# Attention with a gated mixture of experts: the exponentials of the shortest tiles transposed by TensorE, the loads of x placed three units later, four buffers for stored projections

## The chip, the core and the metric

The kernel runs on one NeuronCore of a Trainium2 chip. The core has a matrix engine (TensorE, PE in the profile; PEld is its loading of weights), a vector engine (VectorE, DVE), a scalar engine (ScalarE, ACT), a general engine (GpSimd, POOL) and a queue engine (SyncE, SP). Each works through its own queue of instructions in order. They meet through semaphores only. DMA transfers are issued from the queues of SP, ACT and POOL and run on 16 DMA engines. Matmuls write to PSUM, a memory of eight banks; everything else lies in SBUF or in the chip's main memory (DRAM).

The metric is the device time of one execution in microseconds (us), the median over several. Lower is better. The profile is that of one execution, and all times within it are counted from the start of its span.

## What is computed

```python
xn = layernorm(x)                      # x: (2, 2048, 512), float32
# attention, one head, on xn
x_norm = (xn - mu) / sqrt(var + EPS) * gamma + beta
q, k, v = x_norm @ qkv[:, :512], x_norm @ qkv[:, 512:1024], x_norm @ qkv[:, 1024:]
scores = where(causal, q @ k.T / sqrt(512), -inf)
s = softmax(scores) @ v @ o_proj + xn
# mixture of 8 experts, 2 for each token, on xn (hidden size 352)
top_scores, top_idx = top_k(xn @ gate_w.T + gate_b + bias, 2)
comb = one_hot(top_idx) weighted by softmax(top_scores)
h = silu(xn @ w1[e].T + b1[e]);  y = h @ w2[e].T + b2[e]
g = silu(sum over e of comb[e] * y[e])
return x + s * g
```

## The kernel before

**Stages.** The 4096 tokens are 32 tiles of 128 rows, in eight batches of four. The kernel has three stages, one after the other, all in float32.

The first stage folds the weights (the product of the query and key weights, and that of the value and output weights, L207), normalises each batch (`norm_stats`, `norm_rows`), makes its keys (`keys`, with the transposed rows zT), its gating scores (`both`, `keep_scores`), and from the keys two projections, one for the queries and one for the values. The projections of the first five batches are made by seven products instead of eight (`seven_products`), and those of the last three by plain `unit`s: four matmuls into one of four PSUM banks (`ps_p`), a copy by ScalarE into a buffer of the pool `stg` (L351), and a store to DRAM on ScalarE's queue (L352). Keys and projections go to DRAM. At the end of the stage the tokens are routed (`route`): VectorE counts and sorts with the help of a few small matmuls (L525, L596), with constants that GpSimd has made (from L454 on).

The second stage is the experts: 68 slots of tokens are gathered, transposed by DMA, multiplied (L879), put through silu, transposed, and multiplied again (L918).

The third stage is attention, a loop over steps s. Tile `seq[s]` is the query tile of step s; the causal mask gives it (t + 1) x 128 keys, where t is its place in its sequence of 16 tiles. The order is t = 15, 14, ... 0 for the first sequence and 8, 9, 0, 1, 6, 7, 2, 3, 4, 5, 10 to 15 for the second. `widths[s]` cuts the keys into chunks of up to 512. In step s:

- PE makes the scores of tile s, one PSUM bank of the five of `ps_a` for each chunk (`chunk_scores`, L963). VectorE takes each chunk's maximum (L969), and then nm, the negative of the largest (L981, in `end_scores`).
- ScalarE makes the exponentials pr with nm as bias (`exponentials`, L1035), which also sums them.
- The values of a tile need these exponentials transposed (pT, keys on the partitions). [...]GpSimd copies pr to pu, the two halves of every number apart (L1039); SP issues the DMA transpose (L1044); and in the next step VectorE joins the halves into pT (`join_p`, L1051).
- PE multiplies pT of tile s - 2 with the values (`values`, L1069) in the same step, behind the scores. Some pairs of tiles (`FAST`, the first eight steps' tiles and the last six's) take a form with seven products instead (L1122).
- ScalarE scales the result (`attended`, L1237), VectorE adds to it (L1240), the expert outputs are gathered by GpSimd (`gather_y`, L1216), weighted by VectorE (`gate`, L1227 and L1228) and put through silu by ScalarE (L1232), and GpSimd multiplies and adds (`emit`, L1248 and L1249). Between an exponential and a silu ScalarE loads another table.

**What sets the order.** The whole order is written out by hand: each engine carries out its instructions in the order in which the program text issues them. In the first stage a table, `between`, says after which unit a step of the normalisation comes: `put(at - STEP + 1, norm_rows, b)` places `norm_rows` of batch b. STEP is 6. At its end `norm_rows` issues four DMA loads of x for batch b + 2 on SP's queue (`load`, L160); x has two buffers. Waits come from the buffers: a buffer, a PSUM bank or a place in memory that another tile had before is written only when the last use of that tile is done.

Of the kernel before, what the change touches and what calls it, by code (L numbers as in the profile page):

```python
# [10 lines left out]
F32 = mybir.dt.float32  # L11
# [9 lines left out]
P = 128  # L21
# [5 lines left out]
def gated_attention_moe(  # L27
# [27 lines left out]
    nc = tc.nc  # L55
# [3 lines left out]
    NT = B * S // P  # L59
    BT = 4  # L60
    TB = BT * P
    NB = NT // BT
    NBB = S // TB
# [31 lines left out]
    ident = const.tile([P, P], F32, name="ident")  # L95
# [34 lines left out]
    stage_a = ExitStack()  # L130
    right = lambda st, **k: st.enter_context(tc.tile_pool(side="right", **k))
    psum = lambda st, **k: st.enter_context(tc.tile_pool(space=PSUM, **k))
    kp = right(stage_a, name="kp", bufs=BT)
    mp = right(stage_a, name="mp", bufs=1)
    stg = right(stage_a, name="stg", bufs=3)
    ps_p = psum(stage_a, name="ps_p", bufs=ND)

    wqk = mp.tile([P, ND, D], F32, name="wqk")
# [18 lines left out]
    def load(b):  # L157
        xt = xp.tile([P, BT, D], F32, name=f"x_{b}", tag="x")
        for t in range(BT):
            nc.sync.dma_start(out=xt[:, t, :], in_=xb[:, b * BT + t, :])  # L160
        xin[b] = xt
# [58 lines left out]
    def norm(b):  # L220
        norm_stats(b)
        norm_rows(b)
# [20 lines left out]
    def norm_rows(b):  # L243
        xt = xin.pop(b)
        mv, va, rs = stats.pop(b)
        zs = []
        for t in range(BT):
            z = zp.tile([P, D], F32, name=f"z_{b}_{t}", tag="z")
            nc.vector.tensor_scalar(  # L249
                z, xt[:, t, :], mv[:, t, 0:1], rs[:, t, 1:2], ALU.subtract, ALU.mult  # L250
            )
            zs.append(z)

        ratio = sm.tile([P, BT, 1], F32, name=f"ratio_{b}", tag="ratio", bufs=4)
        nc.vector.tensor_tensor(ratio, va[:, :, 1:2], rs[:, :, 1:2], ALU.mult)
        nc.vector.tensor_tensor(ratio, ratio, rs[:, :, 0:1], ALU.mult)
        nc.vector.tensor_copy(xscale[:, ts(b, BT)], rs[:, :, 0])
        nc.vector.scalar_tensor_tensor(
            xshift[:, ts(b, BT)], mv[:, :, 0], -1.0, rs[:, :, 0], ALU.mult, ALU.mult
        )  # L260
        ratios[b] = ratio
        for t in range(BT):
            zu = zus[t]
            nc.gpsimd.tensor_copy(  # L264
                zu[:, : 2 * D].rearrange("p (h d) -> p h d", h=2),
                zs[t].bitcast(U16).rearrange("p (d h) -> p h d", h=2),
            )
            nc.gpsimd.tensor_copy(zu[:, 2 * D : 2 * D + 2], ratio[:, t, :].bitcast(U16))
            if b >= BY_TE:
                zuT = zup.tile([P, 2 * ND, P], U16, name=f"zuT_{b}_{t}", tag="zuT", bufs=BT + 2)  # L270
                nc.sync.dma_start_transpose(out=zuT, in_=zu[:, : 2 * D])
                zuts[b, t] = zuT
            nc.sync.dma_start(out=zu_rows[:, b * BT + t, :], in_=zu)
        zs_of[b] = zs
        if b + 2 < NB:
            load(b + 2)

    def keys(b):
# [405 lines left out]
    def put(i, f, *args):  # L684
        between.setdefault(i, []).append((f, args))

    STEP = 6
# [3 lines left out]
    for b in range(1, NB):  # L691
        at = LAST - 5 - STEP * (NB - 1 - b) if b > 1 else 1
        put(at, keys, b)
        put(at + 3, both, b)
        put(at + (5 if b == NB - 1 else 7), keep_scores, b)
        if b > 1:

            put(max(at - STEP - 1, 0), norm_stats, b)
            put(at - STEP + 1, norm_rows, b)
    for e in range(E):  # L700
        put(LAST - 5 + e, load_w1, e)

# [249 lines left out]
    widths, scored, halves, turned, sums, gates, outs = {}, {}, {}, {}, {}, {}, {}  # L952
# [38 lines left out]
    ps_a = psum(att, name="ps_a", bufs=5)  # L991
# [13 lines left out]
    for i in range(NS):  # L1005
        experts_step(i)
        if i >= 8 and i % 2 == 0 and early:
            f, b, c = early.pop(0)
# [14 lines left out]
    tp = left(name="tp", bufs=3)  # L1023
# [4 lines left out]
    def exponentials(s):  # L1028

        _, nm, chunks = scored.pop(s)  # L1030
        rs = sm.tile([P, NBB], F32, name=f"rs_{s}", tag="rs")
        sums[s], halves[s] = rs, []
        for j, w in enumerate(widths[s]):
            pr = pp.tile([P, TB], F32, name=f"pr_{s}_{j}", tag="pr")
            nc.scalar.activation(  # L1035
                pr[:, :w], chunks[j][:, :w], AF.Exp, bias=nm, accum_out=rs[:, j : j + 1]
            )
            pu = php.tile([P, 2 * TB], U16, name=f"pu_{s}_{j}", tag="pu")
            nc.gpsimd.tensor_copy(  # L1039
                pu[:, : 2 * w].rearrange("p (h d) -> p h d", h=2),  # L1040
                pr[:, :w].bitcast(U16).rearrange("p (d h) -> p h d", h=2),
            )
            puT = php.tile([P, 2 * BT, P], U16, name=f"puT_{s}_{j}", tag="puT", bufs=5)
            nc.sync.dma_start_transpose(out=puT[:, : 2 * w // P, :], in_=pu[:, : 2 * w])  # L1044
            halves[s].append(puT)

    def join_p(s, j):
        w = widths[s][j]
        if j == 0:
            turned[s] = tp.tile([P, NBB * TB], F32, name=f"pT_{s}", tag="pT")  # L1050
        nc.vector.tensor_copy(  # L1051
            turned[s][:, j * TB : j * TB + w].bitcast(U16).rearrange("p (i t h) -> p i t h", t=P, h=2),
            halves[s][j][:, : 2 * w // P, :].rearrange("p (h i) t -> p i t h", h=2),
        )

    def values(s):
        po = ps_b.tile([P, D], F32, name=f"po_{s}", tag="b")
        product(po, s, 0, place_keys(s), slice(0, D))
        outs[s] = po

    def place_keys(s):

        return place(s)[1] + 1 + (place(s)[0] - place(s)[2]) * BT

    def product(dst, s, k0, k1, cols, start=True):

        first = place(s)[2]
        for k in range(k0, k1):
            nc.tensor.matmul(  # L1069
                dst, lhsT=turned[s][:, ts(k, P)], rhs=avs[first + k // BT][:, k % BT, cols],  # L1070
                start=(start and k == k0), stop=(k == k1 - 1),
            )
# [223 lines left out]
    for s in range(NT + OUT + 2):  # L1296
        fast = s // 2 - 1 in FAST
        if s < NT and s:
            begin_scores(s)
        if s == 1:  # L1300
            fetch_parts(s, 2 * ND)
        for k in range(NT):
            if k not in AHEAD:
                wait = 4 - k % 2 if k // 2 in FAST else 3
                if s == k + wait:
                    attended(k)
                if s == k + wait + 1:
                    emit(k)
        for k in range(NT):
            if s == (NT - 1 if k in AHEAD else k + 2 - k % 2 if k // 2 in FAST else k + 1):  # L1310
                fetch_inputs(k)
        joins = []
        if 0 <= s - 1 < NT - 1:
            joins = [(join_p, s - 1, j) for j in range(len(widths[s - 1]))]
        if s < NT:
            for j in range(len(widths[s])):
                if s:
                    chunk_scores(s, j)
                if joins:
                    f, *args = joins.pop(0)  # L1320
                    f(*args)
                if s == 2 and j:
                    for b in (0, 1) if j == 1 else (j,):
                        combine_v(b, (1,))
        for f, *args in joins:
            f(*args)
        if s < NT and s:
            end_scores(s)
        if fast and s % 2 == 0 and s < NT:
            combine_p(s - 2, range(NBB) if s == 2 else ())  # L1330
        if 0 <= s - 1 < NT:
            divisor(s - 1)
        if s < NT:
            exponentials(s)
            fetch_parts(s, 4 if s else 2 * ND)
            if s in combine:
                combine_v(combine[s])
        if fast and s % 2 == 0:
            values_first(s - 2)

            if s != NT - 2:
                values_next(s - 2)
        elif fast and s == NT - 1:
            values_next(s - 3)
            gate(s - 1)
            values_end(
                s - 3,
                [lambda j=j: join_p(s, j) for j in range(len(widths[s]))] + [lambda: combine_p(s - 1)],
            )
            for k in AHEAD:  # L1350
                make_ahead(k)
        elif fast:
            values_end(s - 3)
        elif 0 <= s - 2 < NT:
            values(s - 2)

        for k in range(0, NT - 2, 2):
            if s == (k + 2 if k + 2 in AHEAD else k + 3):
                gate(k)
        for k in range(0, NT, 2):  # L1360
            if s == (k if k in AHEAD else k + 1):
                gather_y(k)
                gather_y(k + 1)
# [45 lines left out]
```

## Time and profile before

| | |
|---|---|
| Median of 3 runs | 1072.64 us (1067.35, 1072.64, 1072.9) |
| Profiled execution | 1072.68 us, of which the span is 1071.0 |
| PE busy (98% of the span) | 1051.0 us |
| DVE, POOL, ACT busy | 598.7, 422.1, 310.6 us |
| Units of the last three batches | about 177 to 261 us |
| Experts | about 261 to 616 us |
| Steps 12 to 25 of attention | about 806 to 926 us |
| One plain copy of a projection (L351) | 586 ns, 24 of them |
| One copy of pr (L1039) | 1042 ns, 80 of them |
| DMA transpose of pu, issue to landing | 2.3 to 5.8 us, median 3.2 |
| One join (L1051) | 684 ns (283 to 2198), 80 of them |

Busy time is the sum of an engine's instructions. A wait in the profile is idle time of an engine before an instruction, with the one that released it; for instructions with several semaphores it is the one that came last. A float32 matmul is recorded as two, so eight records are four matmuls. Times of PE's ends are modelled: the distance from one start to the next says more than a length.

### The profile page before, as it was taken

How to read it: one execution, taken by the hardware profiler on the slowest of the kernel's cores; microseconds unless marked ns; L12 is line 12 of the kernel's file. 1: busy time of each engine (PE TensorE's matmuls, PEld its weight loads, DVE VectorE, ACT ScalarE, POOL GpSimd, SP SyncE). 2: the span in 40 equal slices, each digit the busy share in tenths (PEclk: the TensorE clock that was granted, in tenths of full speed). 3: DMA queues.
4: the chain of work that ended last, by engine and by line, in shares of the span. 5: the costliest groups of instructions: out<-in, count | busy, mean ns of one | idle time of the engine just before them, and what ended most of it. 6: DMA issues, size and time to landing. Idle time of an engine off the chain costs nothing.

```text
span 1071.0 us, 12108 instructions
## 1 busy us (share of the span) xinstructions
PE 1051.0 (98%) x3566; PEld 620.9 (58%) x3566; DVE 598.7 (56%) x1181; ACT 310.6 (29%) x659; POOL 422.1 (39%) x463
## 2 busy tenths in 40 slices
PE   8999999999999999999999999999999999999998
PEld 3687886444555555555545446776664444446677
DVE  5797884775333333333345338535555667675756
ACT  3212221211322232322355121312333343332330
POOL 2363240003433333333331023244557677574452
PEclk9999999999999999999999999999999999999999
DMA  8599989936999999999985186355668777763451
GB/s 305 170 282 280 276 257 335 351 123 176 225 222 234 226 227 227 232 226 224 214 187 131 42 224 145 91 122 156 154 176 231 219 201 207 202 171 91 108 141 40
DMA packets 303775, 210.11 MB, mean 196 GB/s; under 512 B 237784, under 2 KB 250840, under 8 KB 302688
## 3 DMA queue, kind: packets, MB, share of 16 engines
q1 hardware_dynamic: 284512, 146.91, 55.1%
q0 software_dynamic: 10560, 35.17, 13.1%
q10 hardware_dynamic: 8640, 27.27, 7.1%
q8 instruction: 30, 0.49, 0.2%
q14 instruction: 33, 0.27, 0.1%
HBM read 92.89 MB, written 60.03 MB: 143 GB/s over the span
## 4 chain that ended last, share of the span: by engine, by line
PE 65%; issue 13%; POOL 8%; DMA 5%; DVE 5%; SPq 2%; ACT 2%; ACTq 0%; POOLq 0%; DVEq 0%
PE ph L879 15%; PE py L918 15%; PE ps L963 13%; PE p L1122 10%; PE p L400 5%; PE pw L207 3%; DMA puT<-pu 2%; PE p L1069 2%; POOL yg L1216 2%; POOL pu L1039 1%; DMA zuT<-zu 1%; POOL o L1249 1%; POOL o L1248 1%; PE po L1069 1%; POOL zu L264 1%
## 5 line engine op out<-in xcount | busy, mean ns | idle before, releaser
L963 PE MATMUL ps<-k,q 128*128 128x512 f32 (+3 forms) x640 | 239.1, 529 | 0.0
L963 PEld LDWEIGHTS ps<-k,q 128*128 128x128 f32 x640 | 117.7, 190 | 122.0 <-issue 112.1
L918 PE MATMUL py<-w,ht 128*128 (+3 forms) x408 | 187.0, 594 | 0.0
L879 PE MATMUL ph<-w,xT 128*128 (+1 forms) x544 | 173.2, 460 | 0.7 <-POOL keep L1001 0.7
L1039 POOL COPY pu<-pr 128x1024 uint16<-128x1024 uint16 (+3 forms) x80 | 85.1, 1092 | 176.1 <-ACT pr L1035 158.1
L926 DVE COPY y<-py 128x512 f32<-128x512 f32 x68 | 46.9, 690 | 177.4 <-PE py L918 177.4
L879 PEld LDWEIGHTS ph<-w,xT 128*128 128x128 f32 (+1 forms) x544 | 97.5, 181 | 74.1 <-issue 35.2
L904 ACT ACTIVATE ht<-ht,b1sel 128x128 f32<-128x128 f32 (+3 forms) x237 | 73.1, 375 | 231.8 <-DVE ht L898 231.8
L889 POOL COPY hu<-h 128x704 uint16<-128x704 uint16 x68 | 52.3, 769 | 206.8 <-ACT h L887 145.5
L918 PEld LDWEIGHTS py<-w,ht 128*128 128x128 f32 (+3 forms) x408 | 73.5, 182 | 75.4 <-issue 37.4
L765 POOL DMA_INDIRECT xs<-zu_d,toki x68 | 69.1, 1017 | 75.7 <-DVE toki L642 64.3
L1035 ACT ACTIVATE pr<-ps,nm 128x512 f32<-128x512 f32 (+3 forms) x80 | 49.1, 621 | 151.3 <-DVE ri L1200 136.1
L1069 PE MATMUL po<-v,pT 128*128 128x512 f32 x182 | 82.9, 603 | 5.8 <-DVE ri L1200 3.3
L969 DVE TENSOR_REDUCE mx<-ps 128x1 f32<-128x512 f32 (+3 forms) x80 | 48.6, 608 | 67.3 <-PE ps L963 66.0
L1216 POOL DMA_INDIRECT yg<-y_d,posi x64 | 66.8, 1044 | 38.4 <-DVE g L1227 21.0
L1051 DVE COPY pT<-puT 128x1024 uint16<-128x1024 uint16 (+3 forms) x80 | 61.0, 770 | 25.6 <-DMA puT<-pu 25.4
L264 POOL COPY zu<-z 128x1024 uint16<-128x1024 uint16 x32 | 35.2, 1100 | 80.3 <-DVE z L249 80.3
L1069 PEld LDWEIGHTS po<-v,pT 128*128 128x128 f32 x182 | 34.7, 194 | 45.8 <-issue 43.0
L413 DVE TENSOR_TENSOR so<-p,so 128x512 f32<-128x512 f32 x70 | 46.0, 686 | 15.7 <-PE p L400 7.4
L1240 DVE SCALAR_TENSOR_TENSOR o<-xo,xscale,o 128x512 f32<-128x512 f32 x30 | 27.4, 925 | 47.2 <-ACT o L1237 39.6
L839 DVE COPY xT<-xhT 128x1024 uint16<-128x1024 uint16 x68 | 46.8, 688 | 12.2 <-DMA xhT<-xs 7.1
L1248 POOL TENSOR_TENSOR o<-o,g 128x512 f32<-128x512 f32 x30 | 40.4, 1348 | 14.7 <-DVE o L1240 14.5
(216 smaller groups left out, 1443.8 us busy)
## 6 DMA issues: line engine op xcount, KB each, us to landing
y_d<-y SPq DMA_DIRECT2D x68, 256.0 KB, 3.7
zu_d<-zu SPq DMA_DIRECT2D x32, 264.0 KB, 5.4
x<-in_x_dram SPq DMA_DIRECT2D x32, 256.0 KB, 4.8
kt_d<-kT ACTq DMA_DIRECT2D x8, 1024.0 KB, 6.0
k<-kt_d SPq DMA_DIRECT2D x32, 256.0 KB, 4.4
q<-qt_d SPq DMA_DIRECT2D x32, 256.0 KB, 3.9
v<-v_d SPq DMA_DIRECT2D x32, 256.0 KB, 5.0
xo<-in_x_dram SPq DMA_DIRECT2D x32, 256.0 KB, 3.8
```

The lines of the kernel that those rows point to most:

```text
L400: nc.tensor.matmul(ps[:, r, :], lhsT=lhs[:, c, ts(r, P)], rhs=rhs[:, c, :], start=(c == 0), stop=(c == 1),)
L765: nc.gpsimd.indirect_dma_start(out=xs, out_offset=None, in_=zu_d, in_offset=bass.IndirectOffsetOnAxis(ap=toki[:, i : i + 1], axis=0),)
L879: nc.tensor.matmul(ph[at, :], lhsT=xT[:, c, at], rhs=rhs[k], start=(c == 0), stop=(c == ND - 1),)
L889: nc.gpsimd.tensor_copy(hu[:, :, :H], h.bitcast(U16).rearrange("p (d h) -> p h d", h=2))
L904: nc.scalar.activation(ht[:hn, c, at], ht[:hn, c, at], AF.Silu, bias=b1sel[:hn, c, j : j + 1])
L918: nc.tensor.matmul(py[at, :], lhsT=ht[:k, c, at], rhs=rhs[n], start=(c == 0), stop=(c == NH - 1),)
L963: nc.tensor.matmul(ps[:, :w], lhsT=aqs[seq[s] // 2][:, c, ts(t % 2, P)], rhs=aks[first + j][:, c, :w], start=(c == 0), stop=(c == ND - 1),)
L1039: nc.gpsimd.tensor_copy(pu[:, : 2 * w].rearrange("p (h d) -> p h d", h=2), pr[:, :w].bitcast(U16).rearrange("p (d h) -> p h d", h=2),)
L1051: nc.vector.tensor_copy(turned[s][:, j * TB : j * TB + w].bitcast(U16).rearrange("p (i t h) -> p i t h", t=P, h=2), halves[s][j][:, : 2 * ...
L1069: nc.tensor.matmul(dst, lhsT=turned[s][:, ts(k, P)], rhs=avs[first + k // BT][:, k % BT, cols], start=(start and k == k0), stop=(k == k1 - 1),
L1122: nc.tensor.matmul(dst, lhsT=a[:, k], rhs=v(k), start=(k == 0), stop=(stop and k == n - 1))
L1216: nc.gpsimd.indirect_dma_start(out=y, out_offset=None, in_=y_d, in_offset=bass.IndirectOffsetOnAxis(ap=posi[k][:, n : n + 1], axis=0),)
```

## The change

Three edits.

1. In attention, tiles of at most 384 keys (steps 13, 14, 15, 18, 19 and 22) leave out the copy by GpSimd, the DMA transpose and the join. Their exponentials stay where they are, and PE transposes them block by block with a matmul against the identity into a bank of `ps_a`, behind the values of the tile before; ScalarE copies the bank to pT. The other tiles stay as they are.
2. The loads of x for batch b + 2 (b from 2 on) are no longer issued at the end of `norm_rows`, but by an entry of the table three units later.
3. The pool `stg` has four buffers instead of three.

```diff
-    stg = right(stage_a, name="stg", bufs=3)
+    stg = right(stage_a, name="stg", bufs=4)
...
         zs_of[b] = zs
-        if b + 2 < NB:
+        if b < 2:
             load(b + 2)
...
             put(at - STEP + 1, norm_rows, b)
+            if b + 2 < NB:
+                put(at - STEP + 4, load, b + 2)
...
                 pr[:, :w], chunks[j][:, :w], AF.Exp, bias=nm, accum_out=rs[:, j : j + 1]
             )
+            if by_te(s):
+                halves[s].append(pr)
+                continue
             pu = php.tile([P, 2 * TB], U16, name=f"pu_{s}_{j}", tag="pu")
...
+    def by_te(s):
+        return sum(widths[s]) <= 3 * P
+
+    def turn_p(s):
+        n = sum(widths[s])
+        pt = ps_a.tile([P, TB], F32, name=f"pt_{s}", tag="a")
+        for k in range(n // P):
+            nc.tensor.transpose(pt[:, ts(k, P)], halves[s][0][:, ts(k, P)], ident)
+        turned[s] = tp.tile([P, NBB * TB], F32, name=f"pT_{s}", tag="pT")
+        nc.scalar.copy(turned[s][:, :n], pt[:, :n])
...
-        if 0 <= s - 1 < NT - 1:
+        if 0 <= s - 1 < NT - 1 and not by_te(s - 1):
             joins = [(join_p, s - 1, j) for j in range(len(widths[s - 1]))]
...
         elif 0 <= s - 2 < NT:
             values(s - 2)
+            if s - 1 < NT and by_te(s - 1):
+                turn_p(s - 1)
```

## The prediction

> **What bounds the kernel now.** First the page's busy times, then every wait of the matmul queue over the whole run (who waited for whom: us in total, times, longest).
>
> ```profile
> PE 1051.0 (98%) x3566; PEld 620.9 (58%) x3566; DVE 598.7 (56%) x1181; ACT 310.6 (29%) x659; POOL 422.1 (39%) x463
> ```
> ```profile
> PE po L1069 <- DVE ri L1200: 3.3, 1, 3.3
> PE po L1069 <- DVE pT L1051: 2.5, 3, 1.5
> ```
>
> TensorE sets the end: it idles 20 us of 1071.0, and 5.8 of these are four waits of one line, the product of weights and values (L1069). The rest of the idle time lies in the head, in the tail and before the first tiles of attention. What is not on PE's queue, or does not end one of its waits, is worth nothing. So I read PE's order of time (start, length, work, idle before it and its releaser) around those four waits:
>
> ```profile
> 826.43 1.05 PE L963 MATMUL ps<-k,q 128*128 128x128 f32 x8
> 830.80 4.36 PE L1069 MATMUL po<-v,pT 128*128 128x512 f32 x6 [3.32 <-DVE ri L1200]
> 835.00 7.92 PE L963 MATMUL ps<-k,q 128*128 128x512 f32 x24
> ...
> 855.48 7.99 PE L1069 MATMUL po<-v,pT 128*128 128x512 f32 x18 [0.49 <-DVE pT L1051]
> ...
> 865.71 8.82 PE L1069 MATMUL po<-v,pT 128*128 128x512 f32 x20 [0.51 <-DVE pT L1051]
> ...
> 913.03 2.74 PE L1069 MATMUL po<-v,pT 128*128 128x512 f32 x6
> ...
> 922.39 3.67 PE L1069 MATMUL po<-v,pT 128*128 128x512 f32 x8 [1.46 <-DVE pT L1051]
> ```
>
> The six records at 830.80 are the values of tile 13 (three key blocks, two records each). They wait 3.32 us, and then run slowly: 4.20 us until the next scores start, where the six at 913.03 take 2.58 (next start 915.61). The table of stages (PE, weight loads, DVE, ACT, POOL, granted clock, DMA) shows why:
>
> ```profile
> 830.00:834.00 4.00, 3.20 (x4) 1.51 (x5) 1.58 (x5) 2.52 (x4) 1.52 (x3) 0.57 0.79 293
> 918.00:922.00 4.00, 2.93 (x11) 1.71 (x9) 2.74 (x3) 0.00 (x0) 3.43 (x4) 1.00 0.93 322
> ```
>
> After 3.32 us idle the clock was 0.57; in the wait of 1.46 us it stayed 1.00. So the first wait costs 3.32 + 1.62. All four cost 3.32 + 1.62 + 0.49 + 0.51 + 1.46 = 7.40 us. What ends the first is on VectorE and ScalarE:
>
> ```profile
> 826.55 0.42 DVE L969 TENSOR_REDUCE mx<-ps 128x1 f32<-128x256 f32 x1
> 829.11 1.54 DVE L1051 COPY pT<-puT 128x768 uint16<-128x768 uint16 x1 [2.14 <-DMA puT<-pu]
> 830.58 0.14 DVE L981 TENSOR_REDUCE nm<-mx 128x1 f32<-128x1 f32 x1
> ```
> ```profile
> 830.79 1.28 ACT L1035 ACT_TABLE_LOAD   x1 [5.33 <-DVE ri L1200]
> 832.55 0.77 ACT L1237 ACTIVATE o<-po,xshift,ri 128x512 f32<-128x512 f32 x1
> ```
>
> VectorE holds tile 14's maximum at 826.97, but its in-order queue stands at the join of tile 13 (L1051) until that tile's DMA transpose lands; so the join delays PE, and also nm, the exponential of tile 14, and all behind it.
>
> [...]
>
> **The change by parts.**
>
> *x loaded later.* Sixteen DMAs (four for each of batches 4 to 7) move three units on in the text. In the order of the built program they do not move: on SP's queue they stand behind the same store and before the same transposes, since those three units give SP nothing; every queue and every wait value up to the routing is as before. Zero, with no cover needed.
>
> *Four buffers for stored projections.* In 177 to 261 us ScalarE's copies (L351) waited for their earlier stores 7.5 + 6.7 us, and 6.8 for a load[...]. PE waited for none of it: the copies go through four PSUM banks, and PE runs without a gap from 166 to 261. Zero now; at most the one ACT-bound gap at 261.77, 0.7 us, if the last copy came sooner, which it doesn't (it waits for its matmul). But the buffer shifts the memory of the stage's other pools, and with it a wait: POOL's first routing memset (L454) then waits for the transposes of the last gating scores (L322) instead of the last keys.
>
> ```profile
> 174.85 0.54 POOL L454 MEMSET rank<- 128x32 f32 x8 [16.41 <-ACT kT L295]
> 177.02 0.14 POOL L469 IOTA tile_i<- 128x32 int32 x1
> 180.48 0.60 PE L322 MATMUL pgt<-ident,part 128*128 128x128 f32 x4
> 180.92 7.03 PE L341 MATMUL pj<-kT,wqk 128*128 128x512 f32 x16
> ```
>
> With it go 19 instructions that make constants, 2.3 us; from 181.1 they end at 183.4. VectorE's cast of the last (182.18) comes at about 183.45, so the routing chain is 1.3 us late. Cover: PE reaches the count (L525) at 194.65, the chain is ready at 192.39, leaving 2.2; ScalarE's exp and the copies behind it have 1.9 at the PSUM banks. Zero; without the cover, 1.3.
>
> *Transposes on TensorE.* Tiles 13, 14, 15, 18, 19 and 22 (up to 384 keys; 3, 2, 1, 1, 2, 3 blocks). Removed: six POOL copies (1.30 + 0.61 + 0.40 + 0.86 + 0.61 + 0.91 = 4.7 us), six transposes on SP, six joins on VectorE (1.54 + 0.75 + 0.75 + 0.29 + 1.98 + 0.55 = 5.9 us, and 2.14 + 2.40 of waiting). Added: 12 transposes on PE, (180.92 - 180.48)/4 = 0.11 us each, 1.3 in all, and six ScalarE copies of PSUM, at most the 0.59 of the 512-wide row L351; 0.5 for 384.
>
> New order in step 14: PE does scores 14, values 12, the three transposes (826.43 to 826.76), scores 15 (to 827.6), values 13. ScalarE: table load, exp 14, *copy of tile 13*, o 12. The copy waits behind exp 14, which now needs only the maximum: nm at 826.9 instead of 830.58; table load 827.1 (0.21 later, as now), next instruction 1.76 later as now, 828.85; copy to 829.35; values 13 at 829.45. POOL without the copy of tile 13 (821.34 to 822.64) also frees VectorE: the first L1227 beside it took 1.05 instead of 0.48; I take half of that difference, values 13 at 829.2. PE then idles 1.6 us, nearer to 1.46 (clock held) than to 3.32: I take full clock.
>
> - Values 13 starts 830.80 - 829.2 = 1.6 earlier, and runs 1.62 faster: 3.2.
> - The three small waits: 2.46. Tiles 16, 17 and 23 keep their DMA transposes; what is late is nm, and it moves more than PE: nm 16 follows scores 16 by 4.4 us now, behind joins 14 and 15; without them I get 0.7 (840.7 against scores ending 840.0). So pT 16 is ready about 848 for a PE that comes at 852, and pT 17 about 860 for 861.6. Join 19 no longer waits for DMA (871.6 to 874.0), nm 23 gains about 7 us, and pT 23 is ready at 915 for a PE that comes at 917.
> - Nine transposes after values 13: -0.96.
>
> Sum 3.2 + 2.46 - 0.96 = 4.7 us. After 926 PE has no wait over 0.2 us and the other engines wait for it, so the lead reaches the end. The profiled execution is 1072.68 (1071.0 span and 1.7 around it), and the median of the runs 1072.64: 1068.0.
>
> New waits. The copy waits for PE's transposes, which stand behind the values of the tile before: 8.65 us of them in step 19, where exp 19 is done about 866 and the copy of tile 18 comes at 870.4. Behind it on ScalarE are the gates' silu and o 17; o 17 needs those same values, so nothing later is late, and pT 18 is wanted only after scores 20 (876). The transposes take a bank of the five that scores have: the second chunk of scores 17 (845.3) now waits for exp 16, first chunk (842.7), where the third did before. An exponential keeps its buffer, one of three, until PE has read it: exp 16's third chunk (843.4) waits for the transpose of tile 15 (841.9). All are met by 1.5 us or more.
>
> Bounds of the unknown: [...]The copies' time and the contention: values 13 between 828.6 and 829.8.
>
> **The rivals.** *Nothing left of the waits* (0.17): exp 14 comes so early that values 13 does not wait. For it: DVE and POOL both lose work. Against: silu of the gates ends at 824.8 whatever changes. 7.40 - 0.96 = 6.4: 1066.2. *Waits move* (0.20): the loop nm, exp, o, maximum is the pace of steps 16 to 25, and the clock falls once more. 1.6 - 0.96, and half of 2.46: 1.9 saved, 1070.8. For it: nm trails the scores by 3 to 11 us there. *Slower through ScalarE's order* (0.09): the copy of tile 13 stands behind exp 14 and its table load. If nm 14 stays at 830.58, the copy ends at 833.05 and values 13 starts 2.35 later, at half clock as now, with the transposes on top: +3.3, 1076.0. It decides once nm 14 is later than 829.7: values 13 then starts 1.5 us late, which is what the small waits give less the transposes. Against: the maximum is there at 826.97 and nothing else stands before nm.
>
> **Numbers.** Likeliest 0.54, 1068.0, own range 1066.5 to 1069.5. A measurement of this kernel tells 0.5% (5.4 us) from no change: 1067.3 and 1078.0. Faster by more: the first rival and 0.22 of the likeliest, 0.39. Slower by more: the tail of the last, 0.04. Between, 0.57. Leaving out half of the last rival and the tail of the first: 1064.5 to 1073.5. One of the three runs shown was 1067.35, 5.3 under the others, about one price of the first wait with its slow clock; if that wait is a matter of luck, a median may lie either way.
>
> **What would show it.** Right: no wait of 3 us at values 13, clock 1.00 there, scores 17 starting 2.5 to 3 us earlier, tile 24's values 4 to 5 us earlier, no change up to 820 us. Wrong: a wait of PE on the new copy over 2 us, a clock near half after it, or PE waits on joins of tiles 16, 17, 20 or 23; a gap of PE at 194 us; or waits later than 926 that give the lead back.

## The result, and the profile after

| | Before | After |
|---|---|---|
| Median of 19 runs each | 1072.01 us (1067.35 to 1075.1) | 1065.82 us (1063.15 to 1069.17) |
| Profiled execution | 1072.68 us, span 1071.0 | 1064.85 us, span 1063.1 |
| Ratio to before | | 0.9952, 95% interval 0.9941 to 0.9964 |

The change gains 0.48%, 5.1 us of 1072 (3.9 to 6.3); the two medians are 6.2 us apart, the means 5.2. That is just under the 0.5% at which the prediction divides "faster" from "the same", and the interval has 0.995 inside it; it excludes a ratio of 1. The profiled executions differ by 7.8 us, and not all of that belongs to the change, as will be seen. In the changed kernel the lines of attention stand later in the text: the values' product is L1087, the scores L966, the maximum nm L984, the exponential L1038, the scaling of o L1255 and the addition to it L1258, the weighted gates L1245 and L1246, the join L1069; new are the transposes (L1061) and their copy (L1063).

First the busy times, with 12 matmuls more (the transposes), six ScalarE instructions more (their copies; the table loads are 35 in both, of 1.28 us each) and six fewer on VectorE and on POOL. Then the waits of the matmul queue on the values' product: of four there is one left.

```profile
PE 1047.8 (99%) x3578; PEld 619.9 (58%) x3578; DVE 592.9 (56%) x1175; ACT 312.1 (29%) x665; POOL 419.2 (39%) x457
```
```profile
PE po L1087 <- ACT pT L1063: 1.1, 1, 1.1
```

PE's order of time after the change, around the places shown of before (start, length, work, idle before it and its releaser):

```profile
823.81 0.49 PE L1061 MATMUL pt<-ident,pr 128*128 128x128 f32 x3
824.14 1.06 PE L966 MATMUL ps<-k,q 128*128 128x128 f32 x8
826.34 2.84 PE L1087 MATMUL po<-v,pT 128*128 128x512 f32 x6 [1.14 <-ACT pT L1063]
829.02 0.38 PE L1061 MATMUL pt<-ident,pr 128*128 128x128 f32 x2
829.24 7.92 PE L966 MATMUL ps<-k,q 128*128 128x512 f32 x24
...
848.28 1.05 PE L966 MATMUL ps<-k,q 128*128 128x128 f32 x8
849.17 7.89 PE L1087 MATMUL po<-v,pT 128*128 128x512 f32 x18
...
909.12 5.32 PE L966 MATMUL ps<-k,q 128*128 128x512 f32 x16
914.28 3.60 PE L1087 MATMUL po<-v,pT 128*128 128x512 f32 x8
```

The values of tile 13 wait 1.14 us instead of 3.32, and their six records take 2.68 us to the next start instead of 4.20. Those of tiles 16 and 23 (849.17 and 914.28) no longer wait. The stage table of that product (PE, weight loads, DVE, ACT, POOL, granted clock, DMA) has the clock at 1.00:

```profile
826.34:829.02 2.68, 2.68 (x6) 1.20 (x7) 1.95 (x4) 0.63 (x1) 2.60 (x3) 1.00 0.61 205
```

VectorE and ScalarE in step 14, from the same order of time, with the maximum and the copy:

```profile
823.37 0.42 DVE L972 TENSOR_REDUCE mx<-ps 128x1 f32<-128x256 f32 x1
823.83 0.15 DVE L984 TENSOR_REDUCE nm<-mx 128x1 f32<-128x1 f32 x1
...
825.36 0.47 ACT L1038 ACTIVATE pr<-ps,nm 128x256 f32<-128x256 f32 x1
...
825.82 0.47 ACT L1063 COPY pT<-pt 128x384 f32<-128x384 f32 x1
```

nm of tile 14 now follows its maximum at once. What holds PE is ScalarE: the copy starts 1.52 us after the transposes (824.30), behind exponential 14 and its table load (824.06, 1.28 us).

Where the gain sits: from the end of the values of tile 12 (826.43 before, 823.81 after) to the start of the last product (1066.22 and 1058.03) it is 239.8 us before and 234.2 after, so 5.6 are gained there. Another 2.6 us of lead were there at the start of that stretch: 3.3 us at the routing, of which 0.8 were lost again at the first tiles of attention, in a wait of PE on VectorE (1.29 us at 652.27 before, 2.08 at 649.66 after). They come from the first stage, where PE stands at the gating scores of a batch until VectorE has that batch's transposed rows zT. Before, and then after:

```profile
91.78 1.06 PE L307 MATMUL pg<-zT,gw 128*32 128x512 f32 x8 [2.29 <-DVE zT L290]
92.78 3.37 PE L400 MATMUL p<-kT,wqk 128*128 128x256 f32 x8
```
```profile
90.16 1.06 PE L307 MATMUL pg<-zT,gw 128*32 128x512 f32 x8 [0.66 <-DVE zT L290]
91.15 1.99 PE L400 MATMUL p<-kT,wqk 128*128 128x256 f32 x8
```

In the profile of before, VectorE waited 4.2 us for one DMA transpose to land (zuT), PE waited 2.29 for VectorE, and then, with a granted clock of 0.57 from 92.78 to 95.94, the next eight records took 3.37 us instead of 1.99. In that of after the wait is 0.66, and the clock stays at 1.00 (from 90 to 95.94). Up to 180 us SP's queue issues the same work in the same order in both profiles, so that the loads placed later have moved nothing there; only the fourth buffer shifts memory. So the first question for the experiments is whether this lead is the change's at all.

### The profile page after: what moved, and what is told of

Its sections match the earlier page's. It is cut to its first block, busy times and chain, and to the rows that moved or that the text cites. A ratio compares the mean times of both kernels' runs of the same rounds, so it can differ in the third digit from the quotient of the medians.

```text
span 1063.1 us, 12108 instructions
## 1 busy us (share of the span) xinstructions
PE 1047.8 (99%) x3578; PEld 619.9 (58%) x3578; DVE 592.9 (56%) x1175; ACT 312.1 (29%) x665; POOL 419.2 (39%) x457
## 4 chain that ended last, share of the span: by engine, by line
PE 82%; DMA 4%; issue 4%; POOL 4%; DVE 3%; ACT 2%; SPq 1%; ACTq 0%; POOLq 0%; DVEq 0%
PE ps L966 18%; PE ph L882 15%; PE py L921 15%; PE p L1140 10%; PE p L400 7%; PE po L1087 5%; PE pj L341 3%; PE pj L346 3%; PE pw L207 2%; PE p L1087 2%; DMA puT<-pu 1%; DMA zuT<-zu 1%; POOL yg L1234 1%; POOL pu L1045 1%; DMA v<-v_d 1%
## 5 line engine op out<-in xcount | busy, mean ns | idle before, releaser
L966 PE MATMUL ps<-k,q 128*128 128x512 f32 (+3 forms) x640 | 239.1, 529 | 0.0
L966 PEld LDWEIGHTS ps<-k,q 128*128 128x128 f32 x640 | 117.2, 190 | 119.7 <-issue 109.8
L1045 POOL COPY pu<-pr 128x1024 uint16<-128x1024 uint16 (+2 forms) x74 | 80.0, 1111 | 171.9 <-ACT pr L1038 149.4
L1038 ACT ACTIVATE pr<-ps,nm 128x512 f32<-128x512 f32 (+3 forms) x80 | 49.0, 620 | 148.3 <-DVE ri L1218 126.2
L1087 PE MATMUL po<-v,pT 128*128 128x512 f32 x182 | 81.2, 593 | 1.1 <-ACT pT L1063 1.1
L1069 DVE COPY pT<-puT 128x1024 uint16<-128x1024 uint16 (+2 forms) x74 | 54.2, 740 | 20.0 <-DMA puT<-pu 20.0
L1087 PEld LDWEIGHTS po<-v,pT 128*128 128x128 f32 x182 | 34.2, 190 | 39.5 <-issue 36.1
L1258 DVE SCALAR_TENSOR_TENSOR o<-xo,xscale,o 128x512 f32<-128x512 f32 x30 | 26.9, 906 | 50.0 <-ACT o L1255 43.0
```

The source lines that it names most:

```text
L966: nc.tensor.matmul(ps[:, :w], lhsT=aqs[seq[s] // 2][:, c, ts(t % 2, P)], rhs=aks[first + j][:, c, :w], start=(c == 0), stop=(c == ND - 1),)
L1045: nc.gpsimd.tensor_copy(pu[:, : 2 * w].rearrange("p (h d) -> p h d", h=2), pr[:, :w].bitcast(U16).rearrange("p (d h) -> p h d", h=2),)
L1069: nc.vector.tensor_copy(turned[s][:, j * TB : j * TB + w].bitcast(U16).rearrange("p (i t h) -> p i t h", t=P, h=2), halves[s][j][:, : 2 * ...
L1087: nc.tensor.matmul(dst, lhsT=turned[s][:, ts(k, P)], rhs=avs[first + k // BT][:, k % BT, cols], start=(start and k == k0), stop=(k == k1 - 1),
```

## The experiments

Each kernel was timed beside the kernel before, on the same chip; the chip differs from row to row, so ratios can be compared, and medians only roughly. "Distance" is the stretch named above, from the end of values 12 to the start of the last product, in the profile: it leaves the first stage out. The four columns of waits are those of PE on the values' product in these steps; "-" is under 0.2 us. "Clock" is that of the product at step 13: at "half" its six records take 4.20 to 4.35 us to the next start, with a granted clock of 0.50 in slices of 0.4 us, and at "full" 2.60 to 2.68, with 1.00 in the profiles of after, of loads and buffers alone and of late joins (with loads and buffers alone, it was the product at step 16 that ran as at half clock).

| Kernel | Median us | Ratio (95%) | Distance us | 13 | 16 | 17 | 23 | Clock |
|---|---|---|---|---|---|---|---|---|
| before | 1072.01 | 1 | 239.8 | 3.32 | 0.49 | 0.51 | 1.46 | half |
| before, again | 1071.20 | 1.0001 (0.9989 to 1.0013) | 239.2 | 2.07 | 1.13 | 0.51 | 1.38 | half |
| loads and buffers alone | 1070.93 | 0.9993 (0.9978 to 1.0007) | 239.2 | 1.97 | 2.26 | - | 0.59 | full |
| transposes alone | 1065.74 | 0.9949 (0.9929 to 0.9969) | 234.2 | 1.13 | - | - | - | full |
| only tile 13 | 1068.53 | 0.9967 (0.9950 to 0.9985) | 237.0 | 1.12 | 2.12 | 0.51 | 0.45 | full |
| all but tile 13 | 1068.33 | 0.9970 (0.9960 to 0.9981) | 237.7 | 3.30 | - | - | - | half |
| joins late, no transposes | 1068.34 | 0.9977 (0.9963 to 0.9990) | 236.7 | 3.32 | 0.63 | 0.51 | - | full |
| copy on VectorE | 1064.46 | 0.9950 (0.9935 to 0.9966) | 233.4 | - | - | 0.37 | - | full |
| four tiles | 1066.76 | 0.9963 (0.9950 to 0.9977) | 233.9 | 1.14 | - | - | - | full |
| after | 1065.82 | 0.9952 (0.9941 to 0.9964) | 234.2 | 1.14 | - | - | - | full |
| after, again | 1065.95 | 0.9945 (0.9924 to 0.9966) | 234.2 | 1.11 | - | - | - | full |
| copy on VectorE, again | 1064.10 | 0.9935 (0.9911 to 0.9959) | 233.4 | - | - | 0.35 | - | full |
| tile 13, copy on VectorE, joins late | 1067.31 | 0.9967 (0.9952 to 0.9982) | 234.9 | - | 2.07 | 0.52 | - | full |

### The kernel before, again

No edit.

> The kernel before once more, unchanged. Two readings of the 3.3 us by which the profile of the changed kernel is already ahead at 180 us. Theory (the landing of one transposed input varies from execution to execution): ratio within 0.998 to 1.002, and the start of the last routing transpose, 180.5 us in the first profile, lies anywhere from 176.5 to 181, with or without the 2.3 us wait on zT at 91.8. Rival (the change moved something in the head): the same 2.3 us wait again, and the routing again at 180.5, within 0.5 us.

Measured: 1.0001, so the comparison tells 0.12% from nothing. The wait on zT was 2.6 us and the last routing transposes started at 181.0: near the rival's mark. So this run alone does not decide; the thirteen profiles together say more. With three buffers (four profiles, in which nothing ahead of attention is edited) those transposes start at 178.6 to 181.0, and the longest wait on zT is 1.0 to 2.6 us. With four (nine profiles) they start at 177.2 to 180.2, and the wait is 0.3 to 2.8 us. So the start varies between executions of the same first stage by 2.4 and 3.0 us, about the lead that was to be explained. The two profiles of the kernel before are the only ones in which the clock fell behind this wait (0.57 from 92.78 in the first; a mean of 0.996 over the span in both, where one slow stretch leaves 0.998); that is about half of the 3.3 us.

### Loads and buffers alone

```diff
-    stg = right(stage_a, name="stg", bufs=3)
+    stg = right(stage_a, name="stg", bufs=4)
...
-        if b + 2 < NB:
+        if b < 2:
             load(b + 2)
...
+            if b + 2 < NB:
+                put(at - STEP + 4, load, b + 2)
```

> The x loads three units later and the fourth buffer, without the transposes. Theory (both are worth nothing; they issue the same work with the same waits up to the routing): ratio 0.998 to 1.002, about 1072; in the attention the 3.3 us wait ahead of the values of step 13 and the three small ones as before; the DVE wait on tot_p at the routing 1.1 instead of 2.7 us. Rival (the head gains from them): 3 us faster, ratio 0.997, the zT wait at 91 us below 1 us.

Measured: 0.9993, an interval around 1. The waits of attention are there, though that at 17 is gone and that at 16 longer (the lines of its queue, us in total, times, longest; L1072 is the values' product here; then the product at step 16):

```profile
PE po L1072 <- DVE pT L1054: 2.9, 2, 2.3
...
PE po L1072 <- DVE ri L1203: 2.0, 1, 2.0
```
```profile
853.72 9.69 PE L1072 MATMUL po<-v,pT 128*128 128x512 f32 x18 [2.26 <-DVE pT L1054]
```

That product ran as at half clock at first: 9.52 us to the next start (863.24), where before it takes 7.83 (855.48 to 863.31), with a mean clock of 0.998 over the span.

VectorE's wait on tot_p at the routing is 1.1 us, where the kernel before has 2.7. The two edits are worth nothing that these runs can tell; a gain of up to 0.22% (2.4 us) is within the interval. Neither was run alone, so a small gain of one against a small loss of the other stays possible.

### Transposes alone

The change without the edits of the last section (three buffers, loads as before).

> The six tiles transposed by TensorE, with loads and buffers as before. Theory: the whole gain is here, 5.2 us, ratio 0.995; one wait of about 1.1 us on the ScalarE copy in steps 12 to 25 and none of the joins. Rival (part of the gain comes from loads and buffers): 2 us, ratio 0.998.

Measured: 0.9949, distance 234.2, the same as the whole change. One wait, 1.13 us on the copy, none on a join. The gain is that of the transposes.

### Only tile 13, and all but tile 13

```diff
-        return sum(widths[s]) <= 3 * P
+        return s == 13
```
```diff
-        return sum(widths[s]) <= 3 * P
+        return sum(widths[s]) <= 3 * P and s != 13
```

> The changed kernel, but of the six tiles only that of step 13 is transposed by TensorE. Theory (the waits are separate: the first was 3.3 us and 1.6 us of slow clock, of which 1.1 us stays, and three transposes cost 0.3): 3.3 us faster than before, ratio 0.997; the three waits of 0.5, 0.5 and 1.5 us remain within 0.3 us each, since the maxima of steps 16, 17 and 23 stand behind the same joins as before. Rival (one chain: TensorE that comes sooner waits as much longer for the tiles of 16 and 17): under 1.5 us faster, waits on the joins of 16 and 17 over 2 us together.

> The changed kernel, but the tile of step 13 goes through its DMA transpose and join as before; the other five are transposed by TensorE. Theory (separate parts): the wait ahead of the values of step 13 is back at 2.0 to 3.3 us, those on joins at steps 16, 17 and 23 stay away; 2 us faster than before, ratio 0.998. Rival (a chain, in which the wait at 16 takes up what 13 gives): over 3.5 us faster, ratio below 0.9967, so that the two halves together come to more than the whole.

Measured: both 0.997, 3.5 and 3.2 us, with intervals 3.8 and 2.2 us wide. Neither rival's time was reached, though the first rival's waits were (2.12 + 0.51 us at 16 and 17, where over 2 was its sign). On the sum the times and the profiles do not agree. By the times it is 6.7 us, more than the whole, but uncertain by about 2 us. By the distance it is less: against 239.4 (the mean of the three kernels with all the waits), tile 13 alone gives 2.4 us and the other five give 1.7, where the whole gives 5.2. And a distance is that of one execution, with or without a stretch at half clock, which costs some 1.6 us (4.20 to 4.35 us instead of 2.65 or 2.68 at step 13): those three and "all but tile 13" have one each, "only tile 13" has none. So the sum decides nothing. The waits do: the parts are not separate, and here the first theory missed. In the kernel with tile 13 alone the wait at 16 did not stay at 0.5 us:

```profile
828.40 2.84 PE L1087 MATMUL po<-v,pT 128*128 128x512 f32 x6 [1.12 <-ACT pT L1063]
853.18 7.99 PE L1087 MATMUL po<-v,pT 128*128 128x512 f32 x18 [2.12 <-DVE pT L1069]
```

A PE that comes sooner waits longer for the tile of 16. In the three kernels with all the waits, too, the second grows as the first shrinks: 3.32 and 0.49, 2.07 and 1.13, 1.97 and 2.26 (in the last pair the half clock at 13 is missing too, which in the other two holds PE back as a wait does). The first wait hides part of the second. With the other five tiles transposed and 13 not, only the first is left, at 3.30.

### Joins late, no transposes

```diff
+        late = []
+        if 0 <= s - 1 < NT - 1 and sum(widths[s - 1]) <= 3 * P:
+            late, joins = joins, []
...
             divisor(s - 1)
+        for f, *args in late:
+            f(*args)
```

> The kernel before with every DMA transpose kept; only VectorE's order is changed: the joins of the tiles of up to 384 keys are put behind the maximum and the divisor of the next step instead of ahead of them. Theory (the wait at 13 is the landing of its own tile, the later ones come from maxima that stand behind joins): the wait at 13 is still 2.0 to 3.3 us, with the maximum of step 14 at the end of scores 14 plus 0.5; the joins at 16, 17 and 23 are waited for under 0.5 us in all; 2 us faster, ratio 0.998. Rival (the later waits are landings too, or the late joins hold up the next maxima): within 1 us of before, the waits at 16, 17 and 23 over 1.5 us in all.

Measured: 0.9977, distance 236.7. VectorE, and the product that waits:

```profile
825.65 0.15 DVE L981 TENSOR_REDUCE nm<-mx 128x1 f32<-128x1 f32 x1
...
827.81 1.48 DVE L1051 COPY pT<-puT 128x768 uint16<-128x768 uint16 x1 [1.75 <-DMA puT<-pu]
```
```profile
829.44 2.81 PE L1069 MATMUL po<-v,pT 128*128 128x512 f32 x6 [3.32 <-DVE pT L1051]
```

nm of tile 14 comes 0.58 us after scores 15 start (825.07). That is 4 us after scores 14, not the 0.5 expected, for VectorE's addition to an o (824.19) stands ahead of it; but it no longer stands behind the join. And still the values of tile 13 wait 3.32 us, now on their own join, which begins when its DMA transpose has landed. So the first wait is the landing, and this order of VectorE does not mend it. The wait at 23 is gone, that at 16 and 17 is not (0.63 + 0.51, where under 0.5 was expected).

The clock stayed at 1.00 after those 3.32 us, and that flatters the distance by some 1.6 us against the profiles in which it was half (2.65 us to the next start, where those have 4.20 to 4.35). It does not explain the gain in time. 20 of the 22 runs of this kernel have a mean clock of 0.998 or less over their span, as a run with a stretch at half clock has (see the last section). Taken at 0.998 alone, its 13 runs average 1068.1 us, and the 37 of the kernel before beside it 1070.9. So the order of VectorE alone is worth about 2.8 us, uncertain by about 1: some half of what the whole change gains.

### Copy on VectorE, and again beside the changed kernel

```diff
-        nc.scalar.copy(turned[s][:, :n], pt[:, :n])
+        nc.vector.tensor_copy(turned[s][:, :n], pt[:, :n])
```

> The changed kernel with the copy of the transposed tiles on VectorE in place of ScalarE. Theory (what is left of the first wait, 1.1 us, is the place behind exponential 14 and its table load on ScalarE): the copy of tile 13 starts within 0.7 us of its transposes' end, no wait of values 13, 1.1 us faster than the changed kernel, ratio to before 0.994. Rival (VectorE's own queue holds the copy as long, or the copy there delays maxima): a wait of 1 us or more on the copy or on a join, ratio 0.995 or above.

> The changed kernel once more, on the chip of the two below. Ratio to before 0.995 again, within 0.001. Readings of the head: if the 3.3 us by which its first profile led at 180 us are chance, the last routing transposes start between 176.5 and 181 us, later than 178.5 as likely as not; if they belong to the kernel, at 177.2 within 0.5 us.

> The changed kernel with the copy of the transposed tiles on VectorE, once more, to hold it against the changed kernel on one chip. From the distance between the start of scores 15 and the last product in the profiles, 0.8 us faster than the changed kernel, ratio to before 0.9945. Rival (the time given free at step 13 is taken again by a wait on a join later on): the same as the changed kernel within 0.3 us.

Measured: 0.9950 and 0.9935, medians 1064.46 and 1064.10. In the second profile, VectorE's copy and the product that needs it:

```profile
823.24 0.56 DVE L1063 COPY pT<-pt 128x384 f32<-128x384 f32 x1
823.93 2.76 PE L1087 MATMUL po<-v,pT 128*128 128x512 f32 x6
```

The copy starts 0.04 us after the transposes end (822.71 + 0.49) and PE does not wait. The 1.1 us left of the first wait was the place in ScalarE's queue. A wait of 0.37 and 0.35 us on the join at 17 comes instead, so the distance is 0.8 us shorter than the changed kernel's in both pairs of profiles. By the ratios the version is ahead by 0.2 us (0.9950 against 0.9952) and, on one chip, by 1.1 us (0.9935 against 0.9945). The intervals overlap, and that it is faster is not shown. "After, again" gave 0.9945, and its routing transposes at 178.0.

### Four tiles

```diff
-        return sum(widths[s]) <= 3 * P
+        return s in (13, 14, 15, 22)
```

> The changed kernel, but of the six tiles only those of steps 13, 14, 15 and 22 are transposed by TensorE; 18 and 19 go by DMA as before. Theory (their transposes cost 0.3 us, and no wait of before hangs on them): the same as the changed kernel within 0.5 us, ratio 0.995, no wait on a join over 0.5 us. Rival (they free VectorE for the maxima of steps 20 to 23): a wait on a join of 0.7 us or more between steps 20 and 23 is back.

Measured: 0.9963, distance 233.9 (0.3 less than with six), no wait on a join. By the distance the tiles of 18 and 19 need not go through TensorE. The ratio is 0.0011 above the changed kernel's (1.2 us), and the intervals overlap; the profile has a PE wait of 0.9 us on a ScalarE copy (L351) in the first stage that has nothing to do with these tiles.

### Tile 13 with its copy on VectorE, the other joins late

The edits "only tile 13", "joins late" and "copy on VectorE" together.

> The tile of step 13 alone transposed by TensorE, its copy on VectorE; the other five keep their DMA transposes, with their joins behind the next maximum and divisor. If the first wait and the order of VectorE are all that there is, no wait at 13, about 1 us of waits at 16, 17 and 23 as with the late joins alone, and 1 us less of transposes than in the changed kernel: ratio 0.995, the same as the changed kernel within 0.5 us. Rival (a tile that goes by DMA comes too late for a TensorE that no longer waited at 13): waits of over 2 us on joins, ratio 0.9965 or above.

Measured: 0.9967, the rival's value, and 2.07 us of wait at 16. The distance, 234.9, is only 0.7 us above the changed kernel's. It is that of the fastest of the 22 runs (1064.13 us), in which the clock stayed at full after that wait (a mean of 1.000 over the span); in 11 of them the mean clock is 0.998 or less. VectorE's order of time shows what hangs on tile 14, here with its DMA transpose:

```profile
827.45 0.16 DVE L1219 RECIPROCAL ri<-ri 128x1 f32<-128x1 f32 x1
830.30 0.43 DVE L1069 COPY pT<-puT 128x512 uint16<-128x512 uint16 x1 [2.68 <-DMA puT<-pu]
830.64 0.48 DVE L1245 TENSOR_SCALAR g<-yg,share 128x512 f32<-128x512 f32 x1
...
836.22 2.22 DVE L1258 SCALAR_TENSOR_TENSOR o<-xo,xscale,o 128x512 f32<-128x512 f32 x1 [3.13 <-ACT o L1255]
...
840.21 0.16 DVE L984 TENSOR_REDUCE nm<-mx 128x1 f32<-128x3 f32 x1
```

And the same places in the changed kernel:

```profile
829.24 0.16 DVE L1219 RECIPROCAL ri<-ri 128x1 f32<-128x1 f32 x1
829.33 0.51 DVE L1245 TENSOR_SCALAR g<-yg,share 128x512 f32<-128x512 f32 x1
...
834.93 2.20 DVE L1258 SCALAR_TENSOR_TENSOR o<-xo,xscale,o 128x512 f32<-128x512 f32 x1 [3.13 <-ACT o L1255]
...
838.90 0.16 DVE L984 TENSOR_REDUCE nm<-mx 128x1 f32<-128x3 f32 x1
```

Behind the join of tile 14 stand the weighted gates (L1245, L1246). ScalarE's silu needs these, its o of tile 13 stands behind the silu, VectorE's addition to o behind that, and the maxima of tile 16 behind the addition. In the first kernel VectorE stands 2.68 us for the landing, and nm of tile 16 comes 12.8 us after the reciprocal; in the changed one it does not stand there, and nm comes 9.7 us after it. So tile 14, too, has to leave the DMA if PE comes early, and late joins alone leave waits at 16. No kernel here transposes tiles 13 and 14 alone: that it is 14 and not 15 is read from this order of time, not tested.

## Why the prediction came out as it did

The prediction was 1068.0 and the median is 1065.82, 2.2 us less: inside the whole range, but 0.7 us below the range of the likeliest case. The mechanism was right; terms of the sum were too small, and two statements beside it were wrong. That the result falls under "the same" and not under "faster" is luck, at 0.9952 with the border at 0.995.

**Loads later, zero.** Right within what can be told (0.9993 with the buffers): SP's queue has the same order in both profiles.

**Four buffers, zero, with a shifted wait at the routing.** Right. POOL's constants come behind the last routing transposes (177.18) as worked out, within 0.2 us:

```profile
177.97 0.54 POOL L454 MEMSET rank<- 128x32 f32 x8 [22.85 <-PE pgt L322]
...
180.14 0.16 POOL L469 IOTA tile_i<- 128x32 int32 x1
```

They take 2.3 us, the wait on tot_p fell from 2.7 to 1.1 as the slack was used, and PE reaches the count (L525) 14.17 us after those transposes started, as before. PE ran from them to the experts in 81.3 us in both. In three of the nine profiles with four buffers it took 0.4 to 1.2 us more, in two of them by a wait of 0.5 and 0.9 us on a ScalarE copy (L351); of four with three buffers none took over 0.2 more. So the zero there may be a small loss; the times don't show it.

**The first wait: values 13 starts 1.6 earlier, and 1.62 of slow clock go.** From the end of values 12 to the start of values 13 it was 4.37 us and is 2.53: 1.84. The values' own stretch went from 4.20 to 2.68: 1.52. Together 3.36 against 3.2. The residual wait was 1.14 instead of 1.6, for nm, table load and exponential came 0.4 us sooner: the weighted gate that had run beside POOL's copy for 1.05 us took 0.48 (L1245 at 819.26), and the prediction had counted on half of that difference. The clock stayed at 1.00, as it took.

**The three small waits, 2.46.** All gone, but each was worth more than its listed idle. Two of the starts of before, ahead of the values shown in the prediction:

```profile
853.93 1.05 PE L963 MATMUL ps<-k,q 128*128 128x128 f32 x8
...
915.61 5.32 PE L963 MATMUL ps<-k,q 128*128 128x512 f32 x16
```

From the start of the scores ahead of it to the start of the values it is 1.55 before and 0.89 after at 16, 2.40 and 1.73 at 17, 6.78 and 5.16 at 23: 0.66 + 0.67 + 1.62 = 2.95 us. Beside a wait PE also loses an overlap of some 0.16 us: the scores at 848.28 last 1.05 by the modelled ends, and the values behind them start after 0.89. That is the mis-sized term: 0.5 us. Of the margins by which these waits were to vanish, the one at 17 was too large: 1.6 us were worked out, and with PE 1.1 us earlier (the copy on VectorE) a wait of 0.37 us was there.

**Nine transposes, -0.96.** 0.22 + 0.11 + 0.11 + 0.22 + 0.32 = 0.98, as priced. The ScalarE copies took 0.47 us for 384 (0.5 was taken) and 0.36 for 256.

Sum: 1.84 + 1.52 + 2.95 - 0.98 = 5.3 us where 4.7 was predicted; the distance gives 5.6 against the first profile of before and 5.2 against the mean of three, and the times 5.1. 0.6 of the 2.2 us by which the forecast was high is this; another 0.6 is that the median it started from, of three runs (1072.64), was above that of the 19 (1072.01). The remaining 1 us is the step from the ratio's 5.1 us to the 6.2 between the medians, and inside the interval of the ratio. The signs came a little stronger than forecast: counted from the end of values 12, scores 17 start 3.0 us earlier (2.5 to 3 forecast), and the lead behind values 23 is 5.6 us (4 to 5).

**"No change up to 820 us": wrong in the profile.** The changed kernel's was 3.3 us ahead at 177 us. The runs put this down to the landing of a transposed input and the half clock that followed it; what is left open is whether the fourth buffer, which shifts the stage's memory, adds a little (the means of the routing's start are 179.9 in four profiles and 178.5 in nine).

**nm 16 late "behind joins 14 and 15".** Half right: what stands on VectorE behind join 14 is not only the maximum but the gates, and through ScalarE the addition to o. nm 16 came 1.9 us after PE was through with scores 16 (837.00), where 0.7 was worked out; that was enough. Moving the joins behind the maximum left the wait at 16.

**Rivals.** "Nothing left of the waits" failed by its own sign, a wait of 1.14 us on the copy, though its figure (1066.2) was nearest to the measured time: luck, since the wait it denied was there. That wait lies in the copy's engine: with the copy on VectorE that wait is gone. "Waits move" did not happen with six tiles, but with tile 13 alone it did (2.12 us at 16). "Slower through ScalarE's order": the copy did stand behind exponential 14, and nm was in time, 0.02 us after the transposes' start; the point from which it decides was far away.

## What to carry to other kernels

Ask of a wait whether it ends with the landing of its own data or with a place in a queue: late joins left the first wait whole, while a copy moved to another engine took away the rest of it. Price a wait by the distance between the starts around it, not by its listed idle alone, and price several waits in a row together: the first hides part of the second. And hold two profiles against each other from a point behind the parts that the edit can't touch, because 2.6 us of the 7.8 here came from a DMA's landing (4.16 us of waiting for it) and the half clock after it (3.37 us instead of 1.99). Last, ask what the order alone would give: putting the joins later, without any transpose on TensorE, gave about half of this gain.

## What the runs showed of the hardware

**The clock after a wait of about 2 us or more differs from profile to profile.** The prediction took the slow clock as the price of 3.32 us idle. Its own profile also has half the clock after 2.29 us (at 91.78): 0.50 in each slice of 0.4 us from 93.40 to 96.60. In the thirteen profiles, behind the first wait for weights, there are thirteen waits of PE of 1.97 to 3.32 us. After six the clock was half: 3.32, 2.07 and 3.30 at step 13, 2.26 at step 16, 2.29 and 2.59 in the first stage. After seven it was full: 1.97 and 3.32 at step 13, 2.12 and 2.07 at step 16, 2.42 and 2.84 in the first stage, 2.08 at the first tiles of attention. Step 13, the 2.29 and the 2.08 are read from the granted clock behind the wait, the others from the mean over the span (below), 2.26 also from the 9.52 us above. After no wait of up to 1.82 us did it fall, those of 1.1 us behind transposes among them. The stage table of the kernel with late joins, then of the one with all but tile 13, after waits of 3.32 and 3.30:

```profile
829.40:832.40 3.00, 2.96 (x7) 1.44 (x8) 1.79 (x6) 0.46 (x2) 2.92 (x3) 1.00 1.43 330
```
```profile
828.40:831.40 3.00, 2.98 (x4) 1.41 (x5) 0.59 (x3) 2.52 (x4) 2.27 (x2) 0.52 1.00 363
```

Where slices of 0.4 us show the slow stretch (at 93 us in the first profile, and at step 13 in the three with the clock at half), it lasted about 3.4 us (in the profile of before the clock is 0.66 over the 5 us from 830, which is 3.4 us at 0.50). The length of a wait alone doesn't decide: the clock fell after 2.07 us and stayed at 1.00 after 3.32. What else decides is not shown by these runs.

**Over many executions it can be counted.** Every run of the experiments has the mean clock over its span. It is 0.996 in the two profiles with two slow stretches, 0.998 in the two with one, and 0.999 or 1.000 in the nine with none. Of the 142 runs of the kernel before in the experiments, 136 have 0.998 or less; with late joins, which leave the 3.32 us wait, 20 of 22; of the changed kernel, which has no wait over 1.2 us on the values' product, 5 of 28. So the full clock in the profile with late joins was the exception, and in the kernel before some slow stretch was all but certain. In which place it fell the unprofiled runs don't tell.

**A DMA transpose's landing moves whole microseconds.** The longest wait of PE for zT in the first stage, behind VectorE, which itself waits for such a transpose, was between 1.0 and 2.6 us in the four profiles in which nothing ahead of attention is edited.
